# A gated-scan block with a routed expert layer: gate and routing steps moved to earlier places in a chunk, scatters spread out, expert weights loaded one block in advance

## Chip, cores and metric

The kernel runs on one core of a Trainium2 chip. The metric is the device time of one launch in microseconds (us).

## The reference

The input x has 4 batches of 1024 tokens with 256 features, all in float32. Everything that follows is float32 too.

```
mod = silu(c) @ wmod                       # six rows of 256 per batch: sa, ca, ga, sb, cb, gb
ga, gb: sign kept, magnitude at least 0.25
h  = layernorm(x) * (1 + ca) + sa
hn = rms_scale * h / rms(h) * split_scale
K  = sigmoid(hn @ W_K);  u, gi, go = split(hn @ W_ugg, 3)
s[t] = K[t-1] * s[t-1] + u[t] * sigmoid(gi[t]) * (1 - K[t])      # along the tokens of a batch
x  = x + ga * ((s * sigmoid(go)) @ W_out + h)
h  = layernorm(x) * (1 + cb) + sb
p  = softmax(h @ Wg + bg);  the best two of 8 experts, weights normed to sum 1
x  = x + gb * sum over the two experts of weight * (gelu(h @ W1[e] + b1[e]) @ W2[e] + b2[e])
```

The hidden width of the first part is 512, that of an expert 1024.

## The kernel before

**Two stages.** The first runs over 8 chunks of 512 tokens, two to a batch (the loop over `c_`). It computes the first part of the block, the second layer norm, and the routing, and it writes the second norm's rows beside the gate row gb to a DRAM table `hx`, and x after the first part to the output. The second runs over blocks of 256 (token, expert) pairs of one expert. Each block gathers its tokens' rows from `hx`, multiplies by the expert's W1 (`b_up`) and W2 (`b_down`), and adds the weighted rows to the output by an indirect DMA.

**Order.** The order of instructions on every engine is written out by hand: the program text is the order. An engine runs its instructions in that order and waits where an operand isn't there. Loads and stores by SyncE stand in one queue in program order too, each issued when the semaphores it waits for allow.

**A chunk.** A chunk has four quarters, `project(c_, hc, mid)` for hc 0 to 3. Each makes four products of 512 columns on TensorE (pk, pgi, pu, pgo; L417), their sigmoids on ScalarE, and the scan with what surrounds it on VectorE (L434 to L444), which leaves z. `mid` lists steps put on ScalarE or TensorE after the second sigmoid. Between the quarters stand the steps of other chunks:

- for the next chunk, the first norm and its transposition (`shift`, `a_norm`, `a_mod`, `a_square`, `a_root`, `a_scale`, `a_turn`)
- for the chunk before, the output product and its residual (`o_pe` L454, `o_resid` L467 and the store L470), the second norm (`f_stats`, `f_norm`, `f_mod`, the store `f_store` L498), and `f_swap`, which turns the normed rows for the gate by a VectorE transposition (L514) and a round trip through DRAM (L518, then four loads L525)
- for the chunk before that, the gate `f_gate`: the products `pl` with Wg (L564), a transposition (L572) and the bias (L573)

**Routing.** It is done once per batch. `r_softmax` (L602, L603) and `r_exp` (ScalarE, L606) are followed by `r_first`, the best expert (L611 to L622 with L627 to L631), and `r_second`, the second best and the counts (L627 to L666). `r_rank_pe` makes a token's rank within its expert by three products into `pr` (L673, L676, L680) from `chose`, `earlier` and `ended`, and `r_place` (L686 to L695) makes of it the place in a list. A batch gives 16 scatters of places and payloads to the DRAM table `lists`; they wait in `waiting`, and `drain(n)` puts up to n of them on GpSimd's queue (L584, L586). Before the change `drain` is called four times a chunk with 3, in the last two chunks with 6. In chunk `c_`, `route` is the batch whose last chunk was `c_ - 2`, `placed` the batch whose last chunk was `c_ - 3`. So batch 0 is routed in chunks 3 and 4, batch 1 in chunks 5 and 6, batch 2 in chunk 7 and the first blocks, batch 3 during the blocks.

**Blocks.** Which expert and which stretch of `lists` a block has stands in small tables (`full_table`, `late_table`), read by SyncE (L810). The first 8 blocks take full blocks of batches 0 and 1, the next 8 of all batches, the others the rest. For block j:

- `fetch_entries(j)` loads the list entries (L822)
- `fetch_rows(j)` gathers the rows by them (GpSimd, L830)
- `fetch_weights(j)` loads W1 (L852), the bias b1 (L853), W2 (L854) and b2 (L855), some 2.2 MB together, into one of three places by j modulo 3; the third is the memory of the projection weights and is free only after the last projection
- `b_turn(j)` turns the rows, for block 0 on TensorE (`ptx`, L903), for the others on VectorE (L911)
- `b_up(j)` makes `ph` (L924) with a gelu (L933), `b_down(j)` makes `pye` (L954), adds and scales (L968, L969), and scatters to the output (L941)

`fetch(j)` is called at the start of block j. From block 28 on the fetches are under conditions on the number of blocks (`fetch_used`).

**The passage.** In the last chunk, after quarter 1, the weights of blocks 0 and 1, the entries of blocks 0 to 7 and the rows of blocks 0 and 1 are fetched. `b_turn(0)` stands in the middle of quarter 3:

```python
        if not more:
            fetch_weights(0)
            fetch_weights(1)
            for j in range(NE):
                fetch_entries(j)

            wait_for(BK[0]["ld"], scattered)
            fetch_rows(0)
            fetch_rows(1)
...
        project(c_, 3, [lambda: a_turn(nxt) if more else b_turn(0)])
```

Of the kernel before, what the change touches and what calls it, by code (L numbers as in the profile page):

```python
# [19 lines left out]
def tile_adaln_block(  # L20
# [35 lines left out]
    B, S, D = x.shape  # L56
# [9 lines left out]
    NCH = T // TB  # L66
# [297 lines left out]
    def a_square(c_):  # L364
        u = work.tile([P, TPB, D], F32, tag="u", name=f"u_{c_}", bufs=1)
        X[c_]["u"] = u
        h = X[c_]["h"]
        ss = small.tile([P, TPB], F32, tag="ss", name=f"ss_{c_}")
        X[c_]["ss"] = ss
        for n in range(TPB):  # L370
            nc.scalar.activation(
                u[:, n, :], h[:, n, :], AF.Square, accum_out=ss[:, n : n + 1]
            )
# [13 lines left out]
    def a_skip(c_):  # L387

        h, xb = X[c_]["h"], X[c_]["x"]
        nc.vector.tensor_mul(h, h, wide_row(MDF[c_ // NB][:, 0, :]))  # L390
        nc.vector.tensor_add(xb, xb, h)
# [54 lines left out]
    def o_pe(c_):  # L446
        z, wo = X[c_]["z"], WO[c_ // NB]
        X[c_]["py"] = []
        for q in range(TPB // 2):
            py = ps_y.tile([P, 2, D], F32, tag="y", name=f"pya_{c_}_{q}")  # L450
            X[c_]["py"].append(py)
            for t in range(2):
                for hc in range(HC):
                    nc.tensor.matmul(  # L454
                        py[:, t, :],
                        lhsT=z[hc][:, ts(2 * q + t, P)],
                        rhs=wo[:, hc, :],
                        start=(hc == 0),
                        stop=(hc == HC - 1),
                    )  # L460
# [17 lines left out]
    def f_norm(c_):  # L478
        norm(new_h2(c_), c_)
# [102 lines left out]
    def drain(n: int):  # L582
        for _ in range(min(n, len(waiting))):
            nc.gpsimd.memset(between, 0.0)  # L584
            place, what = waiting.pop(0)
            ins = nc.gpsimd.indirect_dma_start(  # L586
                out=lists[:, :],
                out_offset=IndirectOffsetOnAxis(ap=place, axis=0),
                in_=what,
                in_offset=None,  # L590
                bounds_check=E * T - 1,
                oob_is_err=False,
            )

            for other in scattered:
                tc.declare_no_dep(ins.ins, other.ins, reason="other places")
            scattered.append(ins)

    def r_softmax(b):
        p = R[b]["p"]  # L600
        m = small.tile([P, NT], F32, tag="m", name=f"m_{b}")
        nc.vector.tensor_reduce(m, p, AX.X, ALU.max)  # L602
        nc.vector.tensor_sub(p, p, wide(m))  # L603

    def r_exp(b):
        nc.scalar.activation(R[b]["p"], R[b]["p"], AF.Exp)  # L606
# [62 lines left out]
    def r_rank_pe(b):  # L669
        chose = R[b]["chose"]  # L670
        pr = ps_tr.tile([P, NT + 1, E], F32, tag="tr", name=f"pr_{b}")
        flat = pr[:, :NT, :].rearrange("p n e -> p (n e)")
        nc.tensor.matmul(  # L673
            flat, lhsT=before, rhs=chose.rearrange("p n e -> p (n e)"), start=True, stop=False
        )
        nc.tensor.matmul(  # L676
            flat, lhsT=ones, rhs=R[b]["earlier"].rearrange("p n e -> p (n e)"),
            start=False, stop=True,
        )
        nc.tensor.matmul(pr[:, NT, :], lhsT=ones, rhs=R[b]["ended"], start=True, stop=True)  # L680
        R[b]["pr"] = pr
# [143 lines left out]
    def fetch_rows(j: int, half: bool = False):  # L825

        hb = turns(xpool, 3, [P, HK, 2 * D], F32, "hb", j)
        for t in range(1 if half else HK):
            BK[j]["gathers"].append(
                nc.gpsimd.indirect_dma_start(  # L830
                    out=hb[:, t, :], out_offset=None, in_=hx[: seen(j), :],
                    in_offset=IndirectOffsetOnAxis(ap=BK[j]["ent"][:, t, 0:1], axis=0),
                    bounds_check=seen(j) - 1, oob_is_err=False,
                )
            )
        BK[j]["hb"] = hb

    def fetch_weights(j: int):
        if j >= NJ:
            return  # L840
        wpool = pools["w"]
        e = entry(j, 0, E - 1)
        if j % 3 == 2:
            w1 = proj[:, : KC * F].rearrange("p (k f) -> p k f", k=KC)
            w2 = proj[:, KC * F :].rearrange("p (c d) -> p c d", c=FC)
            b2b = wo_sb[:, 0, :]
        else:
            w1 = turns(wpool, 2, [P, KC, F], F32, "w1", j % 3)
            w2 = turns(wpool, 2, [P, FC, D], F32, "w2", j % 3)
            b2b = turns(wpool, 2, [P, D], F32, "b2b", j % 3)  # L850
        bb = turns(wpool, 3, [P, FC], F32, "bb", j)
        nc.sync.dma_start(out=w1, in_=W1r[e])  # L852
        nc.sync.dma_start(out=bb, in_=b1d[e])  # L853
        nc.sync.dma_start(out=w2, in_=W2r[e])  # L854
        nc.sync.dma_start(out=b2b, in_=b2[ds(e, 1), :].broadcast_to((P, D)))  # L855
        BK.setdefault(j, {}).update(w1=w1, w2=w2, bb=bb, b2b=b2b)
# [4 lines left out]
    def fetch(j: int):  # L861

        if j + 2 in firsts:
            fetch_entries(j + 2)
        if NE < j + 3 < NJ and j + 3 not in firsts:
            fetch_entries(j + 3)
        if j + 2 < NJ:
            fetch_rows(j + 2)
            fetch_weights(j + 2)

    def fetch_used(j: int, half: bool):
# [144 lines left out]
    for c_ in range(NCH):  # L1016
        nxt, prv, old = c_ + 1, c_ - 1, c_ - 2
        more, was, been = nxt < NCH, prv >= 0, old >= 0
        b, part = divmod(c_, NB)

        route = old // NB if been and old % NB == NB - 1 else None
        placed = (c_ - 3) // NB if c_ >= 3 and (c_ - 3) % NB == NB - 1 else None


        if c_ + 3 < NCH:
            load_x(c_ + 3, nc.sync)
        if more:
            shift(nxt)
        project(c_, 0, [lambda: a_norm(nxt)] if more else [])
        drain(6 if c_ + 2 >= NCH else 3)  # L1030
        if more:
            a_mod(nxt)
        if was:
            a_skip(c_)
            o_pe(prv)
            o_resid(prv)
        if placed is not None:
            r_second(placed)
        if part == NB - 1:
            load_mdf(b + 1)  # L1040


        if part == 0 and was:
            scale_out(b)
        if was:
            f_stats(prv)
        project(c_, 1, [lambda: a_square(nxt)] if more else [])
        if c_ == 0:
            first_contents()
        drain(6 if c_ + 2 >= NCH else 3)  # L1050
        if placed is not None:
            r_rank_pe(placed)
        if been:
            f_gate(old)
        if not more:
            fetch_weights(0)
            fetch_weights(1)
            for j in range(NE):
                fetch_entries(j)

# [3 lines that stand above are left out]
        if part == 0:  # L1064
            if c_ == 0:
                setup_ctx.close()
                pools["w"] = ctx.enter_context(tc.tile_pool(name="weights", bufs=2))
            load_gb(b)
            load_mda(b + 1)
        elif c_ == 1:  # L1070
            clear_rows()
            if c_ == 0:
                load_mdf(1)


        if more:
            a_root(nxt)
        if was:
            shift(prv)
        if placed is not None:  # L1080
            r_place(placed)
        if route is not None:
            r_softmax(route)
        if more:
            a_scale(nxt)
        project(
            c_, 2,
            ([lambda: f_norm(prv)] if was else [])
            + ([lambda: r_exp(route)] if route is not None else []),
        )  # L1090
        drain(6 if c_ + 2 >= NCH else 3)
        if part == 0:
            store_gb(b)
        if c_ + 2 < NCH:
            a_stats(c_ + 2)


        if not was:
            a_skip(c_)
            scale_out(b)  # L1100
        if was:
            f_mod(prv)
            f_store(prv)
        project(c_, 3, [lambda: a_turn(nxt) if more else b_turn(0)])
        drain(6 if c_ + 2 >= NCH else 3)
        if was:
            f_swap(prv)
        if route is not None:
            r_first(route)
        if placed == EARLY_B - 1:  # L1110
            tab["e"] = full_table(NE, "e")

# [1 line left out]

    last = NCH - 1
    fetch(0)
    r_second(B - 2)
    b_up(0)
    r_rank_pe(B - 2)
    b_turn(1)  # L1120
# [120 lines left out]
```

## Time and profile before

| | |
|---|---|
| median of three runs | 796.46 us (795.83 to 797.32) |
| the profiled execution | 795.87 us |
| its span, first to last instruction | 794.1 us |
| TensorE busy, and weight loads | 773.7 us (97%), 578.1 us (73%) |
| VectorE, GpSimd, ScalarE busy | 504.7, 292.7, 242.1 us |
| mean granted clock of TensorE | 0.992 |
| DMA moved | 138 MB |
| chunks, passage and first block, other blocks | to 294, to 347, to 784 us of the span |

The profile is of one execution. Times in it are us from the span's start, durations us unless marked ns. Engines are PE (TensorE products), PEld (its weight loads), DVE (VectorE), ACT (ScalarE), POOL (GpSimd) and SP (SyncE); SPq and POOLq are their issue of DMAs. `L454` is a line of the program. A row of the timeline has start, duration, engine, line, operation, what it writes and reads, and how many were merged; in brackets is idle time ahead of it and what ended that. The end of a product is modelled and overlaps the next one by some 0.16 us; the chain of waits has start-to-start times instead. The clock is a share of full speed.

### The profile page before, as it was taken

How to read it: one execution, taken by the hardware profiler on the slowest of the kernel's cores; microseconds unless marked ns; L12 is line 12 of the kernel's file. 1: busy time of each engine (PE TensorE's matmuls, PEld its weight loads, DVE VectorE, ACT ScalarE, POOL GpSimd, SP SyncE). 2: the span in 40 equal slices, each digit the busy share in tenths (PEclk: the TensorE clock that was granted, in tenths of full speed). 3: DMA queues.
4: the chain of work that ended last, by engine and by line, in shares of the span. 5: the costliest groups of instructions: out<-in, count | busy, mean ns of one | idle time of the engine just before them, and what ended most of it. 6: DMA issues, size and time to landing. Idle time of an engine off the chain costs nothing.

```text
span 794.1 us, 10809 instructions
## 1 busy us (share of the span) xinstructions
PE 773.7 (97%) x3279; PEld 578.1 (73%) x3279; DVE 504.7 (64%) x1391; ACT 242.1 (30%) x560; POOL 292.7 (37%) x370
## 2 busy tenths in 40 slices
PE   8999999999999987999999999999999999999995
PEld 5464545464555635888888888888888888888994
DVE  5787877899789955955645654453635454453564
ACT  4434243535344242132312222131222222132231
POOL 2103010106412812256646465543434343343431
PEclk9999999999999998999999999999999999999998
DMA  8411424052222385698839988797877777785781
GB/s 293 106 58 47 134 98 125 27 179 52 76 80 87 81 253 159 199 288 197 233 95 238 231 224 233 226 281 224 230 218 212 199 225 234 211 232 159 226 263 28
DMA packets 116040, 138.13 MB, mean 174 GB/s; under 512 B 25782, under 2 KB 100090, under 8 KB 115968
## 3 DMA queue, kind: packets, MB, share of 16 engines
q1 hardware_dynamic: 97184, 111.46, 44.5%
q0 software_dynamic: 17216, 25.25, 15.9%
q8 instruction: 32, 0.52, 0.3%
q10 hardware_dynamic: 1568, 0.57, 0.3%
q14 instruction: 40, 0.33, 0.2%
HBM read 113.52 MB, written 25.42 MB: 175 GB/s over the span
## 4 chain that ended last, share of the span: by engine, by line
PE 83%; DMA 9%; DVE 2%; issue 2%; SPq 2%; POOL 0%; POOLq 0%; ACT 0%; DVEq 0%
PE pye_False L954 24%; PE ph_False L924 23%; DMA hb<-hx,ent 7%; PE pya L454 7%; PE pu L417 7%; PE pk L417 6%; PE pgo L417 6%; PE pgi L417 6%; PE idle L263 1%; DMA out_dram<-yb_False,ent 1%; SPq L855 1%; PE pta L399 1%; PE pm L290 1%; DMA hb<-hx,ente 1%; PE pl L564 0%
## 5 line engine op out<-in xcount | busy, mean ns | idle before, releaser
L933 ACT ACTIVATE g_False<-ph_False,bb 128x256 f32<-128x256 f32 x248 | 104.0, 471 | 301.8 <-issue 205.3
L911 DVE STREAM_TRANSPOSE xT<-hb 32x128 f32<-32x128 f32 (+1 forms) x576 | 168.9, 293 | 13.3 <-DMA hb<-hx,ent 4.1
L954 PE MATMUL pye_False<-w,g_False 128*128 128x256 f32 x672 | 148.7, 379 | 0.0
L924 PE MATMUL ph_False<-xT,w 128*128 128x256 f32 x672 | 148.6, 379 | 0.0
L924 PEld LDWEIGHTS ph_False<-xT,w 128*128 128x128 f32 x672 | 127.5, 190 | 17.7 <-issue 0.5
L954 PEld LDWEIGHTS pye_False<-w,g_False 128*128 128x128 f32 x672 | 127.5, 190 | 17.7 <-ACT g_False L933 0.2
L941 POOL DMA_INDIRECT out_dram<-yb_False,ent x46 | 73.4, 1596 | 149.8 <-DVE yb_False L969 149.4
L968 DVE TENSOR_TENSOR yb_False<-pye_False,b2b 128x256 f32<-128x256 f32 x42 | 17.8, 424 | 126.2 <-PE pye_False L954 123.2
L586 POOL DMA_INDIRECT lists<-pay,placei x64 | 67.4, 1053 | 27.9 <-DMA ent<-lists 16.3
L924 PE MATMUL ph_False<-xT,proj 128*128 128x256 f32 x320 | 70.7, 379 | 0.0
L954 PE MATMUL pye_False<-proj,g_False 128*128 128x256 f32 x320 | 70.7, 379 | 0.0
L924 PEld LDWEIGHTS ph_False<-xT,proj 128*128 128x128 f32 x320 | 60.8, 190 | 8.3
L954 PEld LDWEIGHTS pye_False<-proj,g_False 128*128 128x128 f32 x320 | 60.8, 190 | 8.3
L830 POOL DMA_INDIRECT hb<-hx,ent x53 | 55.6, 1049 | 22.9 <-issue 20.9
L417 PE MATMUL pu<-hT,proj 128*128 128x512 f32 x128 | 61.9, 607 | 0.0
L417 PE MATMUL pk<-hT,proj 128*128 128x512 f32 x128 | 61.0, 599 | 0.7 <-ACT hT L1011 0.7
L417 PE MATMUL pgo<-hT,proj 128*128 128x512 f32 x128 | 60.2, 592 | 0.0
L417 PE MATMUL pgi<-hT,proj 128*128 128x512 f32 x128 | 60.1, 592 | 0.0
L223 POOL TENSOR_TENSOR rstd_f<-rstd_f,expo 128x4 f32<-128x4 f32 x8 | 8.2, 1023 | 135.9 <-DVE rstd_f L222 135.9
L454 PE MATMUL pya<-wo,z 128*128 128x256 f32 x256 | 56.6, 379 | 0.0
L454 PEld LDWEIGHTS pya<-wo,z 128*128 128x128 f32 x256 | 48.6, 190 | 9.5 <-issue 3.4
L417 PEld LDWEIGHTS pgo<-hT,proj 128*128 128x128 f32 x128 | 24.5, 191 | 31.2 <-issue 27.3
(234 smaller groups left out, 797.6 us busy)
## 6 DMA issues: line engine op xcount, KB each, us to landing
w<-in_L_ffn_W_dram SPq DMA_DIRECT2D x48, 1024.0 KB, 7.0
proj<-in_L_ffn_W_dram SPq DMA_DIRECT2D x24, 1024.0 KB, 7.4
hx<-gb SPq DMA_DIRECT2D x4, 1024.0 KB, 4.5
out_dram<-x SPq DMA_DIRECT2D x8, 512.0 KB, 3.2
hx<-h SPq DMA_DIRECT2D x8, 512.0 KB, 3.1
x<-in_L_attn_x_dram SPq DMA_DIRECT2D x7, 512.0 KB, 4.9
swapped<-u SPq DMA_DIRECT2D x7, 512.0 KB, 2.9
hT<-swapped SPq DMA_DIRECT2D x28, 128.0 KB, 2.6
```

The costliest lines, as they stand in the source:

```text
L223: nc.gpsimd.tensor_tensor(rstd, rstd, expo[:, 0, :], ALU.pow)
L263: nc.tensor.transpose(idle[:, :P], ident, ident)
L417: nc.tensor.matmul(ps, lhsT=w[:, k, col : col + P], rhs=hT[:, k, :], start=(k == 0), stop=(k == KC - 1),)
L454: nc.tensor.matmul(py[:, t, :], lhsT=z[hc][:, ts(2 * q + t, P)], rhs=wo[:, hc, :], start=(hc == 0), stop=(hc == HC - 1),)
L586: ins = nc.gpsimd.indirect_dma_start(out=lists[:, :], out_offset=IndirectOffsetOnAxis(ap=place, axis=0), in_=what, in_offset=None, bounds_ ...
L830: nc.gpsimd.indirect_dma_start(out=hb[:, t, :], out_offset=None, in_=hx[: seen(j), :], in_offset=IndirectOffsetOnAxis(ap=BK[j]["ent"][:, t ...
L911: nc.vector.transpose(to[ts(q, SQ), :, :, ts(i, SQ)], hb[ts(i, SQ), :, :, ts(q, SQ)])
L924: nc.tensor.matmul(ph[:, u, :], lhsT=w1[:, k, ts(fc, P)], rhs=xT[:, k, :n], start=(k == 0), stop=(k == KC - 1),)
L933: nc.scalar.activation(g[:, fc, :n], ph[:, u, :], AF.Gelu_apprx_tanh, bias=bb[:, fc : fc + 1])
L941: return nc.gpsimd.indirect_dma_start(out=out_rows[:n], out_offset=IndirectOffsetOnAxis(ap=at, axis=0), in_=yb, in_offset=None, bounds_che ...
L954: nc.tensor.matmul(py, lhsT=g[:, fc, ts(t, P)], rhs=w2[:, fc, :], start=(fc == 0), stop=(fc == FC - 1),)
L968: nc.vector.tensor_add(yb, py, b2b)
```

## The change

Nothing that is computed changes; instructions change places.

- The gate `f_gate` of the chunk before the last one moves from after quarter 1 to right after the output product and its residual, ahead of quarter 1.
- `r_softmax` moves from ahead of quarter 2 to ahead of quarter 1, `r_exp` from the middle of quarter 2 to that of quarter 1, `r_first` from after quarter 3 to after quarter 2, `r_second` from the next chunk (after its output product) to after quarter 3. For batch 2 it moves from behind the first `fetch` to the end of the last chunk.
- `r_rank_pe` moves from after quarter 1 to ahead of the output product, `r_place` from ahead of quarter 2 to ahead of quarter 1.
- `drain` takes 2 instead of 3, in the last two chunks 4 instead of 6.
- Weights are fetched for block j + 1 in `fetch(j)` up to block 10, which fetches those of 11 and 12, and for j + 2 after that. In the last chunk only block 0's are fetched.

```diff
@@ fetch
             fetch_entries(j + 3)
         if j + 2 < NJ:
             fetch_rows(j + 2)
+
+        if j <= NE + 2:
+            fetch_weights(j + 1)
+        if NE + 2 <= j < NJ - 2:
             fetch_weights(j + 2)
@@ the loop over chunks
+        at_once = 4 if c_ + 2 >= NCH else 2
...
         project(c_, 0, [lambda: a_norm(nxt)] if more else [])
-        drain(6 if c_ + 2 >= NCH else 3)
+        drain(at_once)
         if more:
             a_mod(nxt)
         if was:
             a_skip(c_)
+            if placed is not None:
+                r_rank_pe(placed)
             o_pe(prv)
             o_resid(prv)
-        if placed is not None:
-            r_second(placed)
+        if been:
+            f_gate(old)
...
         if was:
             f_stats(prv)
-        project(c_, 1, [lambda: a_square(nxt)] if more else [])
+        if placed is not None:
+            r_place(placed)
+        if route is not None:
+            r_softmax(route)
+        project(
+            c_, 1,
+            ([lambda: a_square(nxt)] if more else [])
+            + ([lambda: r_exp(route)] if route is not None else []),
+        )
         if c_ == 0:
             first_contents()
-        drain(6 if c_ + 2 >= NCH else 3)
-        if placed is not None:
-            r_rank_pe(placed)
-        if been:
-            f_gate(old)
+        drain(at_once)
         if not more:
             fetch_weights(0)
-            fetch_weights(1)
             for j in range(NE):
                 fetch_entries(j)
...
-        if placed is not None:
-            r_place(placed)
-        if route is not None:
-            r_softmax(route)
         if more:
             a_scale(nxt)
-        project(
-            c_, 2,
-            ([lambda: f_norm(prv)] if was else [])
-            + ([lambda: r_exp(route)] if route is not None else []),
-        )
-        drain(6 if c_ + 2 >= NCH else 3)
+        project(c_, 2, [lambda: f_norm(prv)] if was else [])
+        drain(at_once)
         if part == 0:
             store_gb(b)
         if c_ + 2 < NCH:
             a_stats(c_ + 2)
+        if route is not None:
+            r_first(route)
...
         project(c_, 3, [lambda: a_turn(nxt) if more else b_turn(0)])
-        drain(6 if c_ + 2 >= NCH else 3)
+        drain(at_once)
         if was:
             f_swap(prv)
         if route is not None:
-            r_first(route)
+            r_second(route)
...
@@ after the loop
     fetch(0)
-    r_second(B - 2)
     b_up(0)
     r_rank_pe(B - 2)
     b_turn(1)
```

## The prediction

> **What bounds the kernel now.** The page's busy rows come first: TensorE is busy 97% of 794.1 us. So I looked for the few places where it isn't, in the list of who waited for whom, TensorE alone.
>
> ```profile
> PE ptx L903 <- DMA hb<-hx,ente: 7.4, 1, 7.4
> PE pr L676 <- DVE earlier L653: 0.4, 1, 0.4
> ```
>
> Columns: total us, times, longest. There is one wait worth anything. TensorE's timeline and the table by stage (us, busy time of PE, PEld, DVE, ACT, POOL, then clock, DMA share, GB/s) show what it costs.
>
> ```profile
> 292.69 1.88 PE L417 MATMUL pgi<-hT,proj 128*128 128x512 f32 x4
> 302.00 1.45 PE L903 MATMUL ptx<-ident,hb 128*128 128x128 f32 x4 [7.43 <-DMA hb<-hx,ente]
> 303.24 3.60 PE L417 MATMUL pu<-hT,proj 128*128 128x512 f32 x4
> 308.40 1.89 PE L924 MATMUL ph_False<-xT,w 128*128 128x256 f32 x8
> ```
>
> ```profile
> 294.60:302.00 7.40, 0.00 (x1) 0.03 (x1) 2.26 (x2) 0.60 (x1) 4.63 (x4) 0.86 0.53 148
> 302.00:306.70 4.70, 4.60 (x9) 2.24 (x10) 0.69 (x1) 0.00 (x0) 2.02 (x2) 0.50 0.72 218
> ```
>
> The wait ends at 302.0 and then the clock is 0.50 until 306.7. A full-speed product takes 1.72 us start to start in the chain, so pgi's own time ends at 294.41. From there to the first expert product at 308.40 are 13.99 us. At full speed there would be four transposes (8 take 0.87 us elsewhere: 0.44), pu and pgo (1.72 each), 3.88 in all. The passage from the projections to the experts loses 10.1 us.
>
> Why the rows are late stands in SyncE's issue queue and GpSimd's timeline.
>
> ```profile
> 278.52 0.41 SPq L852 DMA_DIRECT2D w<-in_L_ffn_W_dram  x1
> ...
> 283.01 5.74 SPq L855 DMA_DIRECT2D b2b<-in_L_ffn_b_dram  x1
> 289.51 6.70 SPq L822 DMA_DIRECT2D ente<-lists  x8
> ```
>
> ```profile
> 296.27 1.60 POOL L830 DMA_INDIRECT hb<-hx,ente  x1 [15.99 <-DMA ente<-lists]
> ```
>
> Two weight sets are issued from 278.5 on; the last issue stands 5.74 us in the queue, and only then come the entry lists. They land just before 296.27, the gathers end at about 302.
>
> **The change, part by part.**
>
> *Weights of block 1 leave the queue ahead of the entries.* Block 0's last issue ends at 280.67; by the present spacing (288.75 to 289.51) entry 0 is issued at 281.4 instead of 289.5. It still stands behind block 0's 2.2 MB and a 0.5 MB store in the same queue. Between 279 and 293.5 DMA moved about 4.9 MB, 340 GB/s; 2.75 MB end at about 287 instead of 293.5, some 6.4 us earlier. The rest of the chain keeps its length (293.5 to 302.0), so the transposes can start at 295.6, and TensorE waits 1.2 us (0.5 to 2 by the rate). [...] In this trace the mean of 0.86 over 7.40 us means that it fell some 5.3 us into the gap. [...] So 10.1 becomes 1.2: **8.9 us gained.** Scatters end earlier than the present 276.6 (16 of 1.28 us, started a quarter-chunk sooner), so they don't hold entry 0.
>
> *Routing one slot up.* Softmax and exponential move into the quarter before, with the same two table loads (1.28 us each), so the 1.55 us that VectorE waits for pgo's sigmoid moves along. The first top-1 part (2.13 us: 230.59 to 232.72) now stands ahead of the second layer norm's modulation and f_swap; the second part (3.24 us) comes right behind f_swap, in the chunk's last quarter. Its rank products stand on TensorE ahead of the output product, where nothing else is queued that could pass them.
>
> ```profile
> 229.43 1.24 DVE L514 STREAM_TRANSPOSE u<-h 128x1024 f32<-128x1024 f32 x1
> 230.59 0.18 DVE L611 TENSOR_REDUCE m<-p 128x8 f32<-128x64 f32 x1
> ...
> 242.16 0.21 DVE L627 TENSOR_REDUCE best<-rest 128x8 f32<-128x64 f32 x1
> ...
> 244.27 0.27 DVE L653 TENSOR_TENSOR earlier<-upto,chose 128x64 f32<-128x64 f32 x1
> ```
>
> In the chain of waits TensorE reaches that place at 233.13 (chunk 6):
>
> ```profile
> 233.13 6.91 PE pya L454 x32
> ```
>
> VectorE, followed through chunk 5 with the new order: go's sigmoid now comes late in quarter 1: pgi's at 208.3, four squares (2.1), two table loads and the exponential (2.8), go (0.6), so z at 214.35 where it was 212.17. Quarter 2's z follows 6.4 us later (root, scale and product chain by their present lengths), at 220.75 instead of 221.19; then come statistics, 2.13 us of top-1 and modulation. So f_swap starts at 229.43 - 0.44 + 2.13 = 231.1, `earlier` done at 234.66 (2.38 us after the second part starts at 232.3). TensorE needs it at 233.29: **1.4 us lost**, and the same in chunk 4, whose rows are the same 72.6 us before: 2.8 us. Bounds: zero if VectorE's idle time of 5.5 us in chunk 5 takes up the top-1 part, 2.2 each if no idle time helps. The value taken is by the rows of exactly these instructions. Behind the waiting rank product stand the output product and all of the quarter. After the last projection the top-1 part is out of the way: the 0.4 us wait on `earlier` goes.
>
> *The gate behind the output product.* Same 8 groups of products (0.57 us), moved forward 7 us. They need the turned tile back from DRAM: last load issued at 235.0, landing 2.2 later, 237.2, against 240.0 for the output product's end. Only chunk 5 is the other way round (202.8 plus 2.4 is 205.2, against 204.0), with scatters among its transfers; with two in place of three per slot and 1.4 us of delay before it I take it at nothing, 0 to 1.2. A gain is excluded, since TensorE does the same work and waits for nothing there now.
>
> *Two scatters to a slot.* 64 stay 64, and GpSimd is busy 37%. What stands behind them in its queue are the powers for the norms; fewer scatters ahead only bring these forward, and what waits for them hides under TensorE. Nothing either way.
>
> *One block ahead up to block 10.* SyncE isn't tied to program order by more than its waits. In blocks 1 to 5 it runs on to the next slot as it comes free, so nothing changes. From block 6 on, every set stands behind an entry list that waits for scatters to land. Then block 7's weights are issued where block 8's are now, and so on to block 11:
>
> ```profile
> 411.67 0.37 SPq L852 DMA_DIRECT2D proj<-in_L_ffn_W_dram  x1
> ...
> 424.63 0.37 SPq L852 DMA_DIRECT2D w<-in_L_ffn_W_dram  x1
> ...
> 437.95 0.37 SPq L852 DMA_DIRECT2D w<-in_L_ffn_W_dram  x1
> ...
> 451.52 0.37 SPq L852 DMA_DIRECT2D proj<-in_L_ffn_W_dram  x1
> ...
> 465.25 0.52 SPq L852 DMA_DIRECT2D w<-in_L_ffn_W_dram  x1
> ```
>
> The blocks that now need them start at 417.5, 431.3, 445.1, 458.9, 472.8: 5.8, 6.7, 7.2, 7.4 and 7.5 us. Landings measured for the first and fourth of these very transfers are 5.0 and 7.2; the bias just behind the second took 5.9. [...] By the rows the loads still start half a block early and land with 0.2 to 0.8 us to spare. I take 0.5 us for all, 0 to 6.5 (below).
>
> **The sum.** 8.9 + 0.4 - 2.8 - 0.5 = 6.0 us. The profiled execution took 795.87 us (span 794.1 and 1.8 around it); it would be 789.9, the span 788.1. The median shown is 0.6 above the profiled one: 796.46 - 6.0 = **790.5**.
>
> **The rivals.**
>
> *No wait for ranks.* VectorE takes the top-1 part into its idle time: 8.9 + 0.4 - 0.5 = 8.8 gained, 787.7. For it: 5.5 us idle in chunk 5. Against: none of it lies between the last z and f_swap.
>
> [...]
>
> *Late weights, slower than before.* If first halves land later than the room, block 7 waits for the excess, and each later block adds its own, though an issue shifts only with the block before last: at 9 us the waits come to 3.2 by block 7, 5.0 by 9 and 6.5 by 11. Break-even is near 9.5 us. Landings up to 11.3 us stand in this trace (block 4's, behind another whole set); at 10.5 us it is 11 us: 790.0 + 11 = 801.0. Against: it is these transfers, in this company, that landed in 5.0 to 7.2.
>
> **How the numbers follow.** Forecast (3 to 8 us gained) 0.56; no wait for ranks 0.14; passage stays, around no change, 0.14; late weights 0.16. About 0.2% (1.6 us) is what a measurement here can tell from none. The passage case lies half in faster, half in no change; of late weights 0.03 are no change and 0.13 slower. That gives faster 0.56 + 0.14 + 0.07 = 0.77, same 0.07 + 0.03 = 0.10, slower 0.13. The forecast's own range is 788.4 to 793.4; for 8 in 10 it reaches to most of the no-wait case and past the passage: 786.8 to 796.0.
>
> **What would show it.** After: the wait at ptx under 2.5 us, at clock 1.0 for the pu behind it; entries issued near 281 (later by the earlier losses); two waits of `pr` for `earlier`, about 1.4 us each, ahead of the output product of chunks 4 and 6; no wait of ph for weights above 1 us in blocks 7 to 11; from block 12 on block after block 13.82 us as now. Wrong if ph waits there for w, if pl waits for its turned tile, or if the half clock returns.

## The result, and the profile after

| | before | after |
|---|---|---|
| median, same chip | 796.89 us (795.83 to 797.95, 4 runs) | 789.03 us (788.92 to 789.67, 4 runs) |
| the profiled execution, its span | 795.87, 794.1 us | 789.1, 787.4 us |
| mean granted clock of TensorE | 0.992 | 0.997 |

The ratio is 0.9892 (95%: 0.986 to 0.9923), a gain of 7.9 us by the medians and of 8.6 by the ratio. The two profiled executions differ by 6.8 us, their spans by 6.7. The forecast was 790.5, a gain of 6.0.

First the list of who waited for whom on TensorE after the change (total us, times, longest):

```profile
PE pr L676 <- DVE earlier L653: 0.8, 2, 0.4
...
PE ph_False L928 <- DMA proj<-in_L_ffn_W_dram: 0.7, 1, 0.7
PE pr L673 <- DVE chose L640: 0.6, 2, 0.3
```

The wait of 7.4 us at `ptx` is gone altogether; the predicted remainder of 1.2 isn't there. Of the waits that came instead, two are the rank products, and one is a block waiting for weights. (Lines of the block functions are four higher than before.) TensorE's timeline at the passage:

```profile
296.26 1.45 PE L417 MATMUL pgi<-hT,proj 128*128 128x512 f32 x3
297.55 0.60 PE L907 MATMUL ptx<-ident,hb 128*128 128x128 f32 x4
297.99 1.88 PE L417 MATMUL pu<-hT,proj 128*128 128x512 f32 x4
...
301.47 0.89 PE L928 MATMUL ph_False<-xT,w 128*128 128x256 f32 x3
```

From the end of pgi (297.55, start of the transposes) to the first expert product are 3.92 us, where it was 13.99. The pu behind the transposes takes 1.88 in place of 3.60: the clock stays up (1.00 from 297 to 302). So all of the 10.1 us came back. SyncE's queue and GpSimd show why:

```profile
284.46 7.13 SPq L822 DMA_DIRECT2D ente<-lists  x8
291.88 1.10 POOL L830 DMA_INDIRECT hb<-hx,ente  x1 [8.01 <-DMA ente<-lists]
```

TensorE reaches this place 3.14 us later than before (297.55 against 294.41). Measured against that, the entries are issued at 281.3, the 281.4 of the forecast, and the first gather at 288.7 instead of 296.3, 7.5 us earlier; the forecast had 6.4.

The 3.14 us were lost in the chunks. TensorE and VectorE around the rank products of chunk 6:

```profile
232.46 1.24 DVE L514 STREAM_TRANSPOSE u<-h 128x1024 f32<-128x1024 f32 x1
...
235.24 0.41 PE L673 MATMUL pr<-chose,before 128*128 128x64 f32 x2 [0.34 <-DVE chose L640]
235.70 0.27 DVE L653 TENSOR_TENSOR earlier<-upto,chose 128x64 f32<-128x64 f32 x1
236.02 0.44 PE L676 MATMUL pr<-earlier,ones 128*128 128x64 f32 x2 [0.38 <-DVE earlier L653]
...
236.49 7.15 PE L454 MATMUL pya<-wo,z 128*128 128x256 f32 x32
```

`f_swap` starts at 232.46, `earlier` is done at 235.97, and the output product starts at 236.49. That TensorE waits in two small pieces, 0.34 and 0.38, hides the size: the last projection product begins at 233.02 and needs 1.72, so TensorE was free at 234.74. Chunks 4 and 6 together cost about 2.6 us by the starts of the products; 0.55 of the 3.14 were there from the span's start (first product at 17.91 against 17.36).

Then block 8, whose weights were issued 7.1 us ahead of it:

```profile
417.22 0.37 SPq L852 DMA_DIRECT2D proj<-in_L_ffn_W_dram  x1
...
424.29 1.97 PE L928 MATMUL ph_False<-xT,proj 128*128 128x256 f32 x8 [0.67 <-DMA proj<-in_L_ffn_W_dram]
```

By progress it lost 0.8. The account: passage 10.1, the rank wait after it 0.75 (from the first expert product to the output product 7.57 us where it was 8.32), less 2.6, 0.8 and 0.55. That is 6.9 of a measured 6.7; 0.2 isn't located.

### The profile page after: what moved, and what is told of

Read it like the earlier page. It is cut to its first block, busy times and chain, and to the rows that moved or that the text cites. A ratio compares the mean times of both kernels' runs of the same rounds, so it can differ in the third digit from the quotient of the medians.

```text
span 787.4 us, 10804 instructions
## 1 busy us (share of the span) xinstructions
PE 772.8 (98%) x3279; PEld 577.1 (73%) x3279; DVE 504.3 (64%) x1391; ACT 241.7 (31%) x560; POOL 290.3 (37%) x370
## 4 chain that ended last, share of the span: by engine, by line
PE 83%; DMA 8%; DVE 4%; issue 2%; POOL 1%; ACT 1%; POOLq 0%; DVEq 0%
PE ph_False L928 25%; PE pye_False L958 23%; PE pya L454 7%; PE pk L417 6%; PE pgi L417 6%; PE pu L417 6%; PE pgo L417 6%; DMA hb<-hx,ent 5%; DMA out_dram<-yb_False,ent 2%; PE idle L263 1%; DMA proj<-in_L_ffn_W_dram 1%; PE pm L290 1%; PE pta L399 1%; PE pl L564 1%; DVE s L443 0%
## 5 line engine op out<-in xcount | busy, mean ns | idle before, releaser
L417 PE MATMUL pu<-hT,proj 128*128 128x512 f32 x128 | 60.2, 592 | 0.0
L972 DVE TENSOR_TENSOR yb_False<-pye_False,wo_sb 128x256 f32<-128x256 f32 x20 | 8.5, 424 | 60.4 <-PE pye_False L958 60.3
```

The costliest lines, as they stand in the source:

```text
L417: nc.tensor.matmul(ps, lhsT=w[:, k, col : col + P], rhs=hT[:, k, :], start=(k == 0), stop=(k == KC - 1),)
L972: nc.vector.tensor_add(yb, py, b2b)
```

## The experiments

Every kernel was timed beside the kernel before on its own chip. Numbers across chips are compared by the ratio. Gains in us are differences of medians; a ratio can put them about 1 us higher, inside its interval.

**1. The weights alone.** The kernel before with only the new fetching of weights.

```diff
         if j + 2 < NJ:
             fetch_rows(j + 2)
+        if j <= NE + 2:
+            fetch_weights(j + 1)
+        if NE + 2 <= j < NJ - 2:
             fetch_weights(j + 2)
@@ last chunk
             fetch_weights(0)
-            fetch_weights(1)
```

> The kernel before with the weights' part of the change alone (block 1's set out of the last chunk, one block ahead up to block 10). If the entries' place in SyncE's queue is the cause, the 10.1 us of the passage go as in the changed kernel, block 8 waits some 0.8 us for its weights, and no rank product waits: about 9 us faster than before, faster than the changed kernel by 1 to 2. If the gain needs the routing and scatters moved up (scatters now end at 276.6, which could hold the first entry), less than 7 us faster, with a wait at ptx over 1.5 us.

Measured 789.09 us (788.2 to 789.89), ratio 0.9889 (0.9867 to 0.9911), as much as the whole change. In its timeline the transposes wait 0.91 us, near the forecast's 1.2:

```profile
290.56 1.49 POOL L830 DMA_INDIRECT hb<-hx,ente  x1 [8.83 <-DMA ente<-lists]
294.62 0.30 PE L907 MATMUL ptx<-ident,hb 128*128 128x128 f32 x1
295.83 0.55 PE L907 MATMUL ptx<-ident,hb 128*128 128x128 f32 x3 [0.91 <-DMA hb<-hx,ente]
```

Its expectation had it one or two us ahead of the whole change. By the time it isn't, and by progress only a little: its block 7 starts at 408.60, that of the whole change at 409.65 and, in experiment 12, at 409.19. What it saves in the chunks, where no rank product waits, it loses at the passage (5.1 us in place of 3.9) and at the rank products behind it (0.75). Its entries are issued at 282.88, 1.4 us later against TensorE than in the whole change, because the x store ahead of them goes out 1.45 us later than in the kernel before. Why that store moved was not settled.

**2. The routing alone.** The changed kernel with the old fetching of weights (the reverse of the diff above).

> The changed kernel with the weights fetched as before: gate, routing and scatters alone moved. If these only cost, 1.5 to 2.5 us slower than before (rank waits of 2.6, less the wait of pr after the passage), and ptx waits 7 to 8 us as before. If scatters that end sooner bring the entries, 3 us or more faster than before.

Measured 799.43 us (796.26 to 802.18, 20 runs), ratio 1.0029 (1.0019 to 1.0038): 2.6 us slower, about the rank waits' size. The list of waits is that of the fastest of the twenty:

```profile
PE ptx L903 <- DMA hb<-hx,ente: 5.4, 2, 4.1
PE pr L676 <- DVE earlier L653: 0.8, 2, 0.4
PE pr L673 <- DVE chose L640: 0.6, 2, 0.3
```

The rows were expected to be waited for 7 to 8 us as before; in this execution it is 5.4. TensorE ends pgi 3.5 us later than in the kernel before (297.87 against 294.41), so a part of what it lost in the chunks disappears in a wait that stands there anyway. Where the slower executions lose their time isn't on record.

So the gain is the weights'. The routing, the gate and the scatters together cost 2.6 us by themselves; with the weights, they come to nothing either way (789.09 without them in experiment 1, 789.03 with them).

**3. Only the clock.** The kernel before with 62 transposes of the identity into block 0's tile ahead of the real ones. They are added work, overwritten at once; nothing is left out.

```diff
             pt = ps_tr.tile([P, KC, TK], F32, tag="tr", name=f"ptx_{j}")
+            for _ in range(62):
+                nc.tensor.transpose(pt[:, 0, :P], ident, ident)
```

> The kernel before with 62 transposes of the identity put on TensorE ahead of block 0's transposes, into the tile that these write afterwards, so that TensorE isn't idle while the rows are on their way. The rows come no sooner. If the half clock is the gap's doing, it is about 2.5 us faster than before, at clock 1.0 through the passage. If the clock falls for another reason, no change.

Measured 795.23 us, ratio 0.9969 (0.9947 to 0.999): 1.6 us. The waiting for the rows stays, only the half clock goes (pu at 1.88):

```profile
294.42 6.93 PE L902 MATMUL ptx<-ident 128*128 128x128 f32 x62
302.38 0.30 PE L905 MATMUL ptx<-ident,hb 128*128 128x128 f32 x1 [1.03 <-DMA hb<-hx,ente]
303.30 1.88 PE L417 MATMUL pu<-hT,proj 128*128 128x512 f32 x4
306.74 3.62 PE L926 MATMUL ph_False<-xT,w 128*128 128x256 f32 x16
```

The passage is 12.3 us (294.42 to 306.74), 1.7 shorter, though here the first gather came 1.0 later than in the kernel before. There, from the first transposition to the first expert product were 6.40 us, 2.5 more than the 3.88 at full speed. So of the 10.1 lost, 1.7 to 2.5 were the clock, the other 8 or so the rows.

**4. Only the place in the queue.** Block 1's weights behind the entries, still two blocks ahead everywhere.

```diff
             fetch_weights(0)
-            fetch_weights(1)
             for j in range(NE):
                 fetch_entries(j)

             wait_for(BK[0]["ld"], scattered)
+            fetch_weights(1)
             fetch_rows(0)
```

> The kernel before with one thing changed: block 1's weights are issued behind the entry lists instead of ahead of them, so all weights are still two blocks ahead. If the order in the queue is the cause, 8 to 10 us faster than before, with a ptx wait of 0 to 2 us (the gathers now share the DMA engines with 2.2 MB of weights) and no wait for weights at block 8. If it takes the lower traffic at the passage, less than 5 us faster.

Measured 792.69 us, ratio 0.9936 (0.9912 to 0.9959): 4.2 us, half of what the shorter lead gives.

```profile
289.92 1.09 POOL L830 DMA_INDIRECT hb<-hx,ente  x1 [8.84 <-DMA ente<-lists]
289.99 0.37 SPq L852 DMA_DIRECT2D w<-in_L_ffn_W_dram  x1
295.89 0.30 PE L903 MATMUL ptx<-ident,hb 128*128 128x128 f32 x1 [1.31 <-DMA hb<-hx,ente]
299.13 0.55 PE L903 MATMUL ptx<-ident,hb 128*128 128x128 f32 x3 [2.93 <-DMA hb<-hx,ente]
299.51 3.30 PE L417 MATMUL pu<-hT,proj 128*128 128x512 f32 x4
```

The gather is issued even earlier than in the first experiment (289.92 against 290.56), but block 1's 2.2 MB come right beside it. From the first gather to the last transposes are 9.2 us, there 5.3, and the clock falls (0.50 from 299.8). In the kernel before both sets were through at 293.5, ahead of the first gather at 296.27. So the order alone isn't enough: ahead of the entries block 1's set delays their issue, behind them it delays the gathers. The shorter lead takes it out of the passage.

**5. Ranks later.** The changed kernel with `r_rank_pe` just ahead of `r_place`, behind the output product.

```diff
-            if placed is not None:
-                r_rank_pe(placed)
             o_pe(prv)
...
+        if placed is not None:
+            r_rank_pe(placed)
         if placed is not None:
             r_place(placed)
```

> The changed kernel with one thing moved: the rank products stand behind the output product, residual and gate, just ahead of the placing that needs them, instead of ahead of the output product. If TensorE's waits for the second best expert's counts in chunks 4 and 6 cost what the two traces differ by (2.6 us), about 786.4, 2.6 us under the changed kernel's 789.0, with no wait at pr in the chunks. If VectorE is what bounds these chunks, the time comes back in the output product or the passage, and it stays within 0.5 us of 789.0.

Measured 788.4 us (787.74 to 788.88), ratio 0.9893 (0.9877 to 0.991). The changed kernel has 0.9892 in the result and 0.9906 in experiment 12, so the edit is worth between nothing and 1.0 us, not 2.6. The rank waits are gone from the list, but another line has come:

```profile
PE pl L564 <- DMA hT<-swapped: 1.4, 2, 1.0
```

The gate now waits for its turned tile. In chunk 5 TensorE now starts the output product 1.1 us earlier (197.60 against 198.71), but VectorE's store of the tile goes out only 0.5 earlier (195.67 against 196.15). The rank wait of the chunk before had given the tile that time; it had hidden that the gate was as late. TensorE ends pgi of the last quarter 1.15 us earlier (296.40 against 297.55).

**6. Weights first.** The changed kernel with a block's weights issued ahead of the entry lists up to block 10.

```diff
+        if j <= NE + 2:
+            fetch_weights(j + 1)
         if j + 2 in firsts:
             fetch_entries(j + 2)
...
-        if j <= NE + 2:
-            fetch_weights(j + 1)
         if NE + 2 <= j < NJ - 2:
```

> The changed kernel with one order turned round: in the blocks up to 10 the next block's weights are issued ahead of the entry lists instead of behind them, still one block ahead. If the entry lists, which wait for scatters to land, are what makes the weights of block 8 late, the 0.8 us wait of ph there goes: about 788.2. If that wait is only one execution's chance, 789.0 within 0.4.

Measured 788.97 us, ratio 0.9903 (0.9888 to 0.9919). No wait of `ph` for weights is left in its list, and the time doesn't show it.

**7. Both.** The last two edits together.

> Both of these on the changed kernel: rank products behind the output product, and weights ahead of the entry lists. If the two costs are separate, their sum: about 785.6 (2.6 and 0.8 under 789.0), the fastest here. If one hides behind the other, not below 786.4.

Measured 787.78 us (787.11 to 789.3), ratio 0.9894 (0.9878 to 0.9911); the gate waits 1.4 us as in 5. It is the lowest median of all, yet by its ratio it can't be told from the changed kernel.

**8. Three scatters to a slot.** The changed kernel with the old number.

```diff
-        at_once = 4 if c_ + 2 >= NCH else 2
+        at_once = 6 if c_ + 2 >= NCH else 3
```

> The changed kernel with three and six scatters to a slot as before, instead of two and four. If the number to a slot hides under TensorE either way, 789.0 within 0.5, with the entries issued in the same place. If it matters for what stands behind in GpSimd's queue or for the round trips through DRAM beside it, 1 us or more slower than 789.0.

Measured 797.23 us (794.15 to 798.64), ratio 1.0008 (0.9996 to 1.0019): the whole gain is gone, 8.2 us by the medians and 9.2 by the ratios. The forecast had "nothing either way" for this line. The waits, and the timeline of chunk 5, first of this kernel, then of the changed one:

```profile
PE pl L564 <- DMA hT<-swapped: 5.3, 2, 3.3
...
195.63 0.36 SPq L518 DMA_DIRECT2D swapped<-u  x1
204.20 1.75 SPq L525 DMA_DIRECT2D hT<-swapped  x4
208.49 1.08 PE L564 MATMUL pl<-hT,wg_sb 128*32 128x128 f32 x16 [3.27 <-DMA hT<-swapped]
209.50 3.78 PE L417 MATMUL pk<-hT,proj 128*128 128x512 f32 x4
```

```profile
196.15 0.36 SPq L518 DMA_DIRECT2D swapped<-u  x1
201.24 1.75 SPq L525 DMA_DIRECT2D hT<-swapped  x4
205.71 0.64 PE L564 MATMUL pl<-hT,wg_sb 128*32 128x128 f32 x16
206.29 1.98 PE L417 MATMUL pk<-hT,proj 128*128 128x512 f32 x4
```

From the store of the turned tile to the loads behind it are 8.6 us in place of 5.1. The gate waits 3.27 us, and then the clock is down (0.50 until 214.2): pl 1.08 and pk 3.78 where they take 0.64 and 1.98. Chunk 5's turn costs 6.1 us between two output products (43.88 against 37.78), chunk 7's gate another 2.0 without a fall of the clock. The DMA view of 195 to 206 us (rate in 40 equal slices, then landing times) shows that the store's bytes are not what is late:

```profile
GB/s 4 0 0 0 0 127 350 354 302 238 186 36 7 11 95 90 60 30 8 15 5 6 0 0 0 0 0 0 0 0 0 0 0 0 0 0 19 205 201 261
...
swapped<-u SPq DMA_DIRECT2D x1, 512.0 KB, 8.5
lists<-pay,placei POOLq DMA_INDIRECT x3, 7.1
```

From 201 to 205 nothing moves at all, and the store has landed only at 204.1. Six scatters were issued on both sides of it (190.9 to 197.4), and those in this view take 7.1 us to land. So the store and the scatters beside it are both late to land; the next run tries whether it is the scatters that hold it up.

Their number isn't all. In the kernel before, the same store of chunk 5 had six scatters at the same distances, and came back sooner:

```profile
195.25 0.36 SPq L518 DMA_DIRECT2D swapped<-u  x1
201.50 1.75 SPq L525 DMA_DIRECT2D hT<-swapped  x4
```

That is 6.3 us. With 6.3 here the gate would have waited about 1 us (an estimate: 3.27 less the 2.3). Why it was 8.6 in this execution was not settled.

**9. The scatters elsewhere.** The changed kernel with the same number per chunk, none in slots 0 and 3, four (eight in the last two chunks) in slots 1 and 2.

```diff
-        at_once = 4 if c_ + 2 >= NCH else 2
+        at_once = 8 if c_ + 2 >= NCH else 4
...
         project(c_, 0, [lambda: a_norm(nxt)] if more else [])
-        drain(at_once)
...
         project(c_, 3, [lambda: a_turn(nxt) if more else b_turn(0)])
-        drain(at_once)
```

> The changed kernel with no list scatters in slots 0 and 3, which lie on both sides of the turned tile's way through DRAM, and twice as many (four and eight) in slots 1 and 2. The number per chunk is the same. Theory (with three scatters to a slot the gate waited because scatters ran beside the turned tile's store and held back its landing, 8.5 us in place of about 5): no wait of the gate for the turned tile, the store lands within 4 us, time 788 to 789.5 us. Rival (three or more scatters in any slot cost, by POOL's queue or by the DMA engines): 793 to 798 us.

Measured 792.65 us (791.38 to 793.42), ratio 0.9956 (0.9943 to 0.997). That lies between the two forecasts. The gate waits for nothing, and in chunk 5 the store is back after 3.0 us:

```profile
196.75 0.36 SPq L518 DMA_DIRECT2D swapped<-u  x1
199.71 1.75 SPq L525 DMA_DIRECT2D hT<-swapped  x4
```

So the scatters beside the store are what holds it up. With none near it the way of that store is 3.0 us; with the four just ahead of it 4.8 to 5.1, in the changed kernel and experiments 5 to 7; with six 6.3 in the kernel before and 8.6 in experiment 8. The time did not follow, because the rival is right as well, by another road. Eight scatters in a row hold GpSimd for 10 us, and a power for the norm stands behind them:

```profile
254.18 0.16 DVE L377 TENSOR_SCALAR ss<-ss 128x4 f32<-128x4 f32 x1
...
260.74 1.06 POOL L378 TENSOR_TENSOR ss<-ss,expo 128x4 f32<-128x4 f32 x1
261.83 0.17 DVE L382 TENSOR_SCALAR ss<-ss 128x4 f32<-128x4 f32 x1 [7.43 <-POOL ss L378]
262.75 1.49 PE L399 MATMUL pta<-ident,u 128*128 128x128 f32 x8 [1.76 <-DVE u L385]
```

VectorE had the sum ready at 254.34; the power is made at 260.74, and TensorE waits for what follows. Chunk 6 costs 2.5 us more between two output products (38.58 against 36.11), and a wait of 1.0 at `ptx` comes with it.

**10. All three.** Ranks later, weights first, and the scatters as in 9.

> The kernel with ranks later and weights first, with the scatters kept out of slots 0 and 3 as well. In the kernel with both but the scatters as in the change, the gate waited 1.4 us for the turned tile where the rank wait had covered it, and the time was 787.8 us. Theory: that wait goes, 786 to 787 us. Rival (the wait has another cause, the store's own time beside the rows' store): 787.5 to 788.5 us.

Measured 792.1 us (791.74 to 794.06), ratio 0.9944 (0.9931 to 0.9958). Both forecasts were missed. The gate's wait fell from 1.4 to 0.3 us, as the theory has it; GpSimd's queue took more than that back (the profiled execution is the slowest of five, 794.06 us):

```profile
PE pta L399 <- DVE u L385: 3.0, 1, 3.0
...
PE pl L564 <- DMA hT<-swapped: 0.3, 1, 0.3
```

**11. One block in advance throughout.** This was to see whether the short lead costs anything once 16 more blocks have it.

```diff
-        if j <= NE + 2:
-            fetch_weights(j + 1)
-        if NE + 2 <= j < NJ - 2:
+        fetch_weights(j + 1)
+        if j == (2 * T - E * P) // TK - 1:
             fetch_weights(j + 2)
```

> The changed kernel with the weights one block in advance in every whole block, not only up to block 10. One block of 14 us then has to hold the weights of the next in all of blocks 11 to 26. In the changed kernel's profile this lead costs one wait of 0.7 us in the six blocks that have it. Theory (a set issued in the middle of a block lands within 9 us and the lead is enough): 789 to 791 us, with ffn1 waits below 2 us in all. Rival of the prediction (late weights, landing after the block's end because scatters of the output rows share the DMA engines and SyncE waits in front of them): some 0.5 to 1 us per block, 16 blocks, 797 to 805 us.

Measured 788.85 us (788.6 to 789.1), ratio 0.9904 (0.9889 to 0.9919). Its list of waits has none for weights, so the lead of one block, 14 us, is enough.

**12. The changed kernel again**, beside 9 to 11 on their chip.

> The changed kernel again, beside the three others on one chip, so that differences of 1 us are compared on the same chip. 788.5 to 789.5 us.

Measured 788.73 us (787.42 to 789.28), ratio 0.9906 (0.989 to 0.9921). In this profile block 8 doesn't wait for its weights, so the 0.7 us of the first profile isn't the same in every execution of the program.

## Why the prediction was right

The direction, the cause and the size held. By its own steps:

- **Weights leave the queue ahead of the entries, 8.9 gained.** The mechanism is shown by experiments 1, 2 and 4. The issue time of the entries was met within 0.1 us. The term was 1.2 too small: the wait of 1.2 is 0.9 in the kernel with the weights alone and 0 in the changed one. What was mis-sized is the 6.4 us by which the first gather comes earlier: it came 7.5 earlier. The step read 4.9 MB at 340 GB/s for 279 to 293.5; the DMA view of that stretch has 4.69 MB at 323 GB/s, by which one set of 2.23 MB is worth 6.9. The bytes were through 7.1 us earlier by TensorE's progress (289.5 less 3.14, against 293.5), and the gather followed them 0.3 sooner. From the first gather to the transposes "the rest of the chain keeps its length" held: 5.7 us before, at most that after, 5.3 in experiment 1.
- **The clock.** The step read 5.3 us into the gap off the mean clock of 0.86, and the sum didn't depend on it, since no gap was left. The runs have since shown that it is no safe limit: falls came 2.2 to 2.8 us after TensorE stopped (below).
- **Rank products ahead of the output product, 2.8 lost.** Measured 2.6 by progress; experiment 2 is 2.6 slower by the medians. VectorE's idle time did not take it up. The rival without that wait falls. But that the 2.8 could be had back was not in the text, and experiment 5 shows that most of it can't: 1.4 of it turns into the gate's wait, and at most 1.0 comes back.
- **The rank wait after the last projection, 0.4 gained.** 0.75 measured.
- **The gate moved, taken at 0.** True in the changed kernel, and true for a reason the step only half gave. It named chunk 5 as the tight one and "two in place of three" as the help, but priced it 0 to 1.2. Experiment 8 puts the price without that help at 8 us, in part by a store that was slower there than the same scatters made it in the kernel before.
- **Two scatters to a slot, "nothing either way".** This step failed. It looked for who waits for GpSimd and didn't ask whose transfers are held up by the scatters beside them: the gate's tile, 8.6 us on its way in place of 5.1. The line isn't a gain by itself; it is what makes moving the gate free. With three to a slot the change would have ended at no change at all (1.0008).
- **One block ahead, 0.5 lost.** 0.8 in one profile, none in another of the same program, and nothing in experiment 11 with 16 more blocks. The true value is near 0. The rival of late weights falls: the only waits for a set in any list are those of block 8, 0.7 us here, 0.2 in experiment 5 and 0.4 in 8.

The sum was 1.9 us short of the medians' 7.9. 1.2 of it is the passage, 0.35 the rank wait after it, 0.5 the weights, 0.2 the ranks. Added, these come to 2.25, so 0.35 went elsewhere; the later start in the profiled execution (0.55) could be it.

No version beat the changed kernel by more than its interval. Keeping both sides of the turned tile's way free without long runs of scatters on GpSimd (the powers put ahead of them, for instance) was not tried. It could be worth, as an estimate, the 1.4 us of waits in experiment 7.

## What to carry to other kernels

When loads are late, look at what stands ahead of the small index loads in their queue and what runs beside the gathers: here a prefetch of 2.2 MB made one block too early cost 8 us, and prefetching later cost nothing. When a step is moved towards its input, look at how long that input's round trip is under the traffic of its new neighbours, and take the wait that is removed as cover for the next one. An edit that looks free can be what another edit rests on: undo each line alone before calling it idle.

## What the hardware showed that was not expected

**A store came back later with scatters around it.** 512 KB to DRAM came back after 3.0 us with no scatters near, 4.8 to 5.1 with four, 6.3 and 8.6 with six, and in experiment 8 some 3 us after the last of its bytes. That the scatters beside it are the cause is shown by experiment 9. How they hold it up is not shown. How much it costs isn't set by their number: in chunk 7 of the kernel before, with twelve scatters within 8 us, the store took 4.6.

**The clock fell after shorter gaps than the prediction took.** In the kernel before it fell 5.3 us after TensorE stopped. In experiments 8 and 10 gaps of 3.27 and 3.02 us were enough. First two rows of the table by stage of experiment 8, where TensorE stopped at 205.22, then experiment 10, where it stopped at 259.2; one row per us (us, busy time of PE, PEld, DVE, ACT, POOL, clock, DMA share, GB/s):

```profile
205.00:206.00 1.00, 0.22 (x2) 0.00 (x0) 1.00 (x3) 0.00 (x0) 0.00 (x0) 1.00 0.72 188
...
207.00:208.00 1.00, 0.00 (x0) 0.00 (x0) 0.00 (x0) 0.00 (x0) 0.00 (x0) 0.69 1.02 262
```

```profile
261.00:262.00 1.00, 0.00 (x0) 0.00 (x0) 0.66 (x4) 0.00 (x0) 0.83 (x3) 0.99 0.00 0
262.00:263.00 1.00, 0.81 (x4) 0.63 (x5) 1.00 (x5) 0.00 (x0) 0.83 (x3) 0.50 0.00 0
...
265.00:266.00 1.00, 1.00 (x3) 0.42 (x2) 0.90 (x2) 0.00 (x0) 0.81 (x3) 0.80 0.02 1
```

The mean of 0.69 puts the fall in experiment 8 at 207.4, 2.2 us after the stop. In experiment 10 it came at 262.0, 2.8 us after the stop, and the clock stayed down 3.4 us. Gaps of 2.0 us (experiment 8, chunk 7) and 1.76 us (experiment 9) left it up.

Whether their length alone parts these gaps from the others is not shown. In the traces' record of the clock, the stretches between the first switch and the last are 293.55 us up, 6.83 down and 481.28 up in the kernel before, and 774.83 up in the changed one: each is a whole multiple of 3.413 us (86, 2, 141 and 227 times). By the tables by stage it was down for 6.8 us in experiment 8 and for 3.4 in 10, two and one of these. In the 3.4 us that ended with the fall TensorE was busy 0 us in the kernel before, 0.6 in experiment 10, 0.7 in 4 and 1.2 in 8. In the kernel before, the 3.4 us ahead of those had 1.5 us of work, and the clock stayed up. For a forecast, a gap from about 2.2 us on is at risk, as an estimate from the fall in experiment 8.
